# Second attention of a conv-attention hybrid: the mirrored blocks of a chunk's own square turned on VectorE and through memory, and turned tiles stored in pieces and loaded in whole rows

## The chip, the cores and the metric

One core of a Trainium2 chip runs the kernel. The metric is the device time of the program in microseconds (us). TensorE (PE) multiplies matrices, VectorE (DVE), ScalarE (ACT) and GpSimd (POOL) work on tiles, and SyncE (SP) issues most DMAs. Each engine runs its own instructions in order.

## The reference

The input x is 8 batches of 128 channels by 48 x 48 = 2304 positions, in float32. The part that matters here is the second attention; it follows a causal first attention and comes before a recurrent layer.

```python
def _L1_attn_ref(x):                      # x: (8, 2304, 128), normed over its 128 channels
    attn = jnp.einsum('bnd,bmd->bnm', x / TEMPERATURE, x)
    attn = jax.nn.softmax(attn, axis=-1)
    out = jnp.einsum('bnm,bmd->bnd', attn, x)
    return out

x = x + _L0_conv_ref(_gn(x), ...)         # projections, causal attention
t = _to_tokens(x)
t = t + _L1_attn_ref(_ln_t(t))            # the second attention
t = t + _L1_ffn_ref(_ln_t(t), ...)        # batch norm, then a recurrence over positions
```

Queries and keys of the second attention are the same vectors, so its score matrix is symmetric: the score of (n, m) is the score of (m, n). The exponential uses one constant shift for all rows, so the exponentials are symmetric too.

## The kernel before

The 2304 positions of a batch are 6 chunks (`NQ`) of 384 columns (`QC`), and each chunk is 3 blocks (`QB`) of 128. The class `Full` makes the second attention. For a chunk j it takes items: a "direct" item m computes scores of the 128 keys of block m against the chunk's 384 queries (L1214), takes the exponential on ScalarE (L1216, which also adds up each row into `rows`), and multiplies the result `p` into the chunk's output in PSUM, `o` (L1228).

Chunks use the symmetry between one another. A direct item of a later chunk n > j is also turned: VectorE transposes `p` in squares of 32 x 32 into a tile `t` (L1177). After three blocks the tile is complete; its column sums go to `tsum` (L1185), and it is stored in memory (`store`, L1157, one DMA in rows of 4608 bytes) and later loaded back with the squares put in their places (`load`, L1148, four DMAs in pieces of 1152 bytes). When chunk n is worked on, the loaded tile `g` gives a "turned" item, which needs no score and no exponential, only its product (L1224). The three blocks of a chunk's own square (n = j) are all direct, with 384 columns each, and aren't turned. `items` lists the items of each chunk in order: for chunk 0 its own blocks first, for later chunks the blocks behind first and the own ones last, with turned items spread among them.

The products follow the scores by three items (`LAG`). Work around this stream (group norm, projections, the end of a chunk) is written as chains of steps. A planner, `Stream`, keeps estimated times of TensorE, VectorE, ScalarE and GpSimd and puts each step into the instruction stream once its estimated time has come (`tick`); `finish` and `advance` force steps earlier and `finish` moves the planner's clock. The first three items of the next batch's causal attention are placed between the last items of chunk 5.

At the end of a chunk, `after` copies `o` out and adds a chain: `sums` forms the softmax denominators from `rows` and, for chunks with later ones behind them, from `tsum` through a small matmul `ts` (L1259) and the mask `mine`; `residual` turns the result back by TensorE, divides, adds and takes moments; further steps normalize and store.

Buffers that matter: 6 for `p`, 2 for `t`, 3 for `g`, one for `ta` (the causal attention's turned sums) and one for `toc` (the causal attention's output after its way through memory, `token_major`, L961 and L967).

Of the kernel before, what the change touches and what calls it, by code (L numbers as in the profile page):

```python
# [604 lines left out]
def fast_path(ctx: ExitStack, tc: tile.TileContext, x, pe, w_ffn, out, x_tok, w_qkv, w_pos, v_t, gamma_beta, flag):  # L605
    nc = tc.nc
# [57 lines left out]
    with ExitStack() as actx:  # L664
# [91 lines left out]
        for r in range(1 - R, R):  # L756
# [3 lines left out]
        mine = apool.tile([P, NQ - 1, R, QB], F32, tag="mine", name="mine")  # L760
        nc.gpsimd.memset(mine, 1.0)
        nc.gpsimd.affine_select(
            out=mine, in_=mine, compare_op=ALU.is_ge, fill=0.0, base=0, pattern=[[0, NQ - 1], [-SQ, R], [0, QB]], channel_multiplier=1
        )
        nc.gpsimd.affine_select(
            out=mine, in_=mine, compare_op=ALU.is_ge, fill=0.0, base=SQ - 1, pattern=[[0, NQ - 1], [SQ, R], [0, QB]], channel_multiplier=-1
# [351 lines left out]
        class Full:  # L1118
# [13 lines left out]
            def items():  # L1132
                chunks = []
                for j in range(NQ):
                    behind = list(range(j + 1, NQ))
                    ahead = [("direct", QB * n + g) for n in ([0] + behind if j == 0 else behind + [j]) for g in range(QB)]
# [3 lines left out]
                    chunks.append([w for _, w in sorted(both, key=lambda e: e[0])])  # L1140
                return listed(chunks)

            def load(self):
                i, j = self.pairs[len(self.loaded)]
                d, _ = self.stored[i, j]
                g = gpool.tile([P, R, QB, QB, SQ], F32, tag="g", name=f"g_{self.b}_{i}_{j}")
                for r in range(R):
                    nc.sync.dma_start(  # L1148
                        g[ts(r, SQ)].rearrange("c a j m r -> c a (j m r)"),
                        d.rearrange("(a c) b f -> b c a f", a=R)[r],  # L1150
                    )
                self.loaded[i, j] = g

            def store(self):
                j, n, t, at = self.to_store.popleft()
                d = dpool.tile([P, R, QB * QB * SQ], F32, tag=f"e_{j}_{n}", name=f"e_{self.b}_{j}_{n}")
                nc.sync.dma_start(d, t.rearrange("p b j m r -> p b (j m r)"))  # L1157
                self.stored[j, n] = d, max(at, st.now)

            def prefetch(self):  # L1160
# [3 lines left out]
                if n < len(self.pairs) and n < self.used + 3 and self.pairs[n] in self.stored:  # L1164
                    if self.stored[self.pairs[n]][1] + 6.0 <= st.now:
                        self.load()

            def turned(self, j, m, p, ready):
# [12 lines left out]
                if g == QB - 1:  # L1181
                    self.to_store.append((j, n, t, at))
                    if j not in self.tsum:
                        self.tsum[j] = small2.tile([P, NQ - 1, R * QB], F32, tag="tsum", name=f"tsum_{b}_{j}")
                    nc.vector.tensor_reduce(  # L1185
                        self.tsum[j][:, n - j - 1, :], t.rearrange("p b j m r -> p (b j) (m r)"), AX.X, ALU.add
# [4 lines left out]
            def begin(self, j, what, first):  # L1191
# [12 lines left out]
                if what[0] == "turned":  # L1204
# [5 lines left out]
                    return self.loaded[i, j][:, :, g, :, :].rearrange("p a m r -> p m a r"), 0.0  # L1210
                m = what[1]
                xh = x_hat[b][1]
                s = psum_s(f"s1_{b}_{j}_{m}")
                nc.tensor.matmul(s[:, :QC], xh[:, ts(m, P)], xh[:, ts(j, QC)], start=True, stop=True)  # L1214
# [418 lines left out]
```

## Time and profile before

| what | value |
|---|---|
| median of 3 runs | 1776.05 us (1774.83 to 1778.08) |
| span of the profiled execution, first to last instruction | 1772.5 us |
| the profiled execution's own time | not listed; the runs' median is 3.6 us above its span |
| mean granted TensorE clock | 0.993 |
| TensorE busy | 1742.7 us (98%) |
| VectorE busy | 1302.8 us (74%) |
| ScalarE busy | 764.8 us (43%) |
| GpSimd busy | 195.2 us (11%) |
| DMA queue with most traffic | 257.47 MB, 49.4% of 16 engines |

Engines work side by side, so busy times don't add up. In the profile's groups, a line of the kernel stands with its engine, its operation, its output and inputs, the count, the busy time, the mean length of one instruction in ns, and the engine's idle time before them with what ended it. A float32 matmul appears as two MATMUL instructions. Matmuls overlap in the records, so the step from one start to the next tells what one costs in a full stream. The chain of work that ended last is followed back from the last instruction.

### The profile page before, as it was taken

To read this page: it belongs to the slowest core of one execution; us is meant where nothing else is said; L and a number is where in the kernel's file an instruction comes from. 1 tells how busy PE (TensorE), PEld (TensorE's weight loads), DVE (VectorE), ACT (ScalarE), POOL (GpSimd) and SP (SyncE) were. 2 spreads that over 40 slices of the span, in tenths; PEclk is the share of its full clock that TensorE was granted. 3 is DMA by queue.
4 is the path that set the end of the run, shared out by engine and by line. 5 is a ranking of instruction groups with operands and counts; after the bars stand their busy time and mean duration, and the time that the engine had idled before them with its cause. 6 is when DMAs were issued, how large, how long until landed. Compare 5 with 4: busy or idle time off the path is not lost.

```text
span 1772.5 us, 22223 instructions
## 1 busy us (share of the span) xinstructions
PE 1742.7 (98%) x6231; PEld 1093.2 (62%) x6231; DVE 1302.8 (74%) x3363; ACT 764.8 (43%) x1842; POOL 195.2 (11%) x303
## 2 busy tenths in 40 slices
PE   8999999999999999999999999999999999999996
PEld 5666566665666566665666656665666656665565
DVE  4868668876887668786687767876687866877467
ACT  2344434443345434444344433454344543444455
POOL 1110011100110001100111001100011001110006
PEclk8999999999999999999999999999999999999998
DMA  4405672257533584156732575335941468116768
GB/s 140 138 23 187 182 204 94 87 184 188 145 103 128 159 226 141 34 176 182 200 99 80 188 192 152 106 111 161 237 129 50 160 183 214 45 65 198 194 211 216
DMA packets 206056, 262.00 MB, mean 148 GB/s; under 512 B 90113, under 2 KB 175010, under 8 KB 205412
## 3 DMA queue, kind: packets, MB, share of 16 engines
q1 hardware_dynamic: 204972, 257.47, 49.4%
q0 software_dynamic: 720, 2.62, 1.0%
q8 instruction: 52, 0.85, 0.2%
q14 instruction: 80, 0.66, 0.1%
q10 hardware_dynamic: 232, 0.40, 0.1%
HBM read 150.24 MB, written 110.17 MB: 147 GB/s over the span
## 4 chain that ended last, share of the span: by engine, by line
PE 96%; DMA 1%; DVE 1%; ACT 0%; issue 0%; SPq 0%; POOL 0%; ACTq 0%; POOLq 0%; DVEq 0%
PE o L1228 18%; PE s L1214 18%; PE s L1013 17%; PE o L1024 17%; PE o L1224 13%; PE pj L874 4%; PE pj L877 2%; PE z L1547 2%; PE wx L1320 2%; PE of_t L934 1%; PE tb L934 1%; PE pb L832 0%; DMA x<-in_x_dram 0%; PE dn L1072 0%; PE ts L1259 0%
## 5 line engine op out<-in xcount | busy, mean ns | idle before, releaser
L1216 ACT ACTIVATE p<-s,shift 128x384 f32<-128x384 f32 x504 | 292.4, 580 | 479.7 <-PE s L1214 464.2
L1015 ACT ACTIVATE p<-s 128x384 f32<-128x384 f32 (+2 forms) x504 | 231.8, 460 | 424.8 <-PE s L1013 377.5
L1214 PE MATMUL s<-xh 128*128 128x384 f32 x1008 | 410.4, 489 | 0.0
L1228 PE MATMUL o<-p,xhT 128*128 128x384 f32 x1008 | 404.1, 488 | 5.9 <-ACT p L1216 5.9
L1013 PE MATMUL s<-q,k 128*128 128x384 f32 (+2 forms) x1008 | 381.5, 460 | 0.2 <-DVE k L884 0.2
L1024 PE MATMUL o<-p,vT 128*128 128x384 f32 (+2 forms) x1008 | 377.4, 456 | 0.0
L1224 PE MATMUL o<-g,xhT 128*128 128x384 f32 x720 | 281.3, 488 | 1.1 <-DMA g<-e 1.1
L1228 PEld LDWEIGHTS o<-p,xhT 128*128 128x128 f32 x1008 | 188.9, 190 | 133.8 <-ACT p L1216 10.5
L1024 PEld LDWEIGHTS o<-p,vT 128*128 128x128 f32 x1008 | 188.8, 190 | 114.7 <-issue 0.6
L1214 PEld LDWEIGHTS s<-xh 128*128 128x128 f32 x1008 | 186.2, 190 | 115.3
L1013 PEld LDWEIGHTS s<-q,k 128*128 128x128 f32 x1008 | 182.6, 191 | 97.3 <-issue 1.0
L1039 DVE TENSOR_TENSOR acc<-acc,p 128x384 f32<-128x384 f32 (+2 forms) x408 | 208.8, 512 | 33.4 <-POOL p L1018 8.7
L1177 DVE STREAM_TRANSPOSE t<-p 128x384 f32<-128x384 f32 x360 | 187.3, 550 | 37.6 <-ACT p L1216 32.8
L1224 PEld LDWEIGHTS o<-g,xhT 128*128 128x128 f32 x720 | 133.2, 190 | 83.7 <-DMA g<-e 1.3
L1185 DVE TENSOR_REDUCE tsum<-t 128x12 f32<-128x1152 f32 x120 | 162.3, 1353 | 4.2
L879 DVE TENSOR_TENSOR z<-pj,pb 128x384 f32<-128x384 f32 x144 | 78.8, 547 | 108.8 <-PE pj L874 92.4
L1018 POOL TENSOR_TENSOR p<-p,triu 128x128 f32<-128x128 f32 x144 | 72.5, 505 | 606.2 <-ACT p L1015 475.2
L1294 POOL TENSOR_TENSOR roots<-ve_f,mhalf 128x3 f32<-128x3 f32 x48 | 40.7, 849 | 521.8 <-DVE ve_f L918 521.8
L1216 ACT ACTIVATION_READ_ACCUMULATOR p<-s,shift 128x1 f32 x504 | 97.2, 193 | 0.0
L874 PE MATMUL pj<-xn,wT 128*128 128x384 f32 x192 | 79.7, 500 | 1.4 <-DVE xn L867 1.4
L924 POOL TENSOR_TENSOR rs_c<-ve_c,mhalf 128x3 f32<-128x3 f32 x48 | 45.1, 939 | 216.2 <-DVE ve_c L918 213.6
L1321 DVE TENSOR_TENSOR scale<-wx,scale 128x384 f32<-128x384 f32 x46 | 25.4, 551 | 56.1 <-PE wx L1320 50.3
(264 smaller groups left out, 1485.6 us busy)
## 6 DMA issues: line engine op xcount, KB each, us to landing
e<-t SPq DMA_DIRECT2D x120, 576.0 KB
g<-e SPq DMA_DIRECT2D x480, 144.0 KB
pb<-posb_d SPq DMA_DIRECT2D x46, 576.0 KB
t1t<-in_x_tok_dram SPq DMA_DIRECT2D x48, 192.0 KB
t_d<-tt SPq DMA_DIRECT2D x184, 48.0 KB
t2x<-t_d SPq DMA_DIRECT2D x46, 192.0 KB
scale<-rs SPq DMA_DIRECT2D x46, 192.0 KB
x<-in_x_dram SPq DMA_DIRECT2D x14, 576.0 KB
```

Of the source, the lines that this page charges most:

```text
L874: nc.tensor.matmul(ps[:, :QC], wT[:, j, :], xn, start=True, stop=True)
L879: nc.vector.tensor_add(z, ps[:, :QC], c["pb"][:, j, :])
L1013: nc.tensor.matmul(s[:, off:QC], keys[b][:, ts(m, P)], queries[b, j][:, off:], start=True, stop=True)
L1015: nc.scalar.activation(p[:, off:], s[:, off:QC], AF.Exp, scale=SCALE)
L1024: nc.tensor.matmul(o[:, off:QC], vals[b][:, ts(m, P)], p[:, off:], start=first, stop=last)
L1039: nc.vector.tensor_add(a[:, off:], a[:, off:], p[:, off:])
L1177: nc.vector.transpose(t[:, :, :, g, :].rearrange("p b j r -> p j b r"), p.rearrange("p (j b r) -> p j b r", j=QB, b=R))
L1185: nc.vector.tensor_reduce(self.tsum[j][:, n - j - 1, :], t.rearrange("p b j m r -> p (b j) (m r)"), AX.X, ALU.add)
L1214: nc.tensor.matmul(s[:, :QC], xh[:, ts(m, P)], xh[:, ts(j, QC)], start=True, stop=True)
L1216: nc.scalar.activation(p, s[:, :QC], AF.Exp, bias=shift, accum_out=self.rows[:, m, j : j + 1])
L1224: nc.tensor.matmul(out_ap, xhT[:, QB * i + g, :], p, start=first, stop=last)
L1228: nc.tensor.matmul(o[:, :QC], xhT[:, what[1], :], p, start=first, stop=last)
```

## The change

Within a chunk's own square the kernel now computes only the blocks on and behind the diagonal. Own block g gets scores and exponentials for the columns from 128 g on (`offset`): 384, 256 and 128 columns. What lies across the diagonal is obtained by turning: `mirror` transposes the 256 columns of block 0 and the 128 of block 1 in squares of 32 into a tile `tm` (the buffer of `ta`), adds up their columns into `tsum`, stores `tm` in memory and loads it back in four pieces into `gm` (the buffer of `toc`). Two "mirrored" items at the end of the chunk multiply `gm` into the first 128 and 256 columns of `o`.

The own blocks move ahead of the blocks behind in every chunk, and each chunk's first direct item comes first, since it opens the accumulation with its full width. `tsum` has one entry more (the own square), `mine` is one wider, and the last chunk now has the `ts` matmul too.

For the turned tiles of later chunks, the putting in place moves from the load to the store: four stores in pieces of 1152 bytes, and one load in rows of 4608 bytes.

```diff
             def items():
                 chunks = []
                 for j in range(NQ):
-                    behind = list(range(j + 1, NQ))
-                    ahead = [("direct", QB * n + g) for n in ([0] + behind if j == 0 else behind + [j]) for g in range(QB)]
+                    ahead = [("direct", QB * n + g) for n in range(j, NQ) for g in range(QB)]
                     turn = [("turned", i, g) for i in range(j) for g in range(QB)]
                     both = [((k + 0.5) / len(ahead), w) for k, w in enumerate(ahead)]
                     both += [((k + 0.5) / len(turn), w) for k, w in enumerate(turn)]
-                    chunks.append([w for _, w in sorted(both, key=lambda e: e[0])])
+                    order_of = [w for _, w in sorted(both, key=lambda e: e[0])]
+                    first = order_of.index(ahead[0])
+                    order_of.insert(0, order_of.pop(first))
+                    chunks.append(order_of + [("mirrored", g) for g in range(1, QB)])
                 return listed(chunks)
+
+            @staticmethod
+            def offset(j, m):
+                return max(0, m - QB * j) * P if m < QB * (j + 1) else 0
 
             def load(self):
...
-                for r in range(R):
-                    nc.sync.dma_start(
-                        g[ts(r, SQ)].rearrange("c a j m r -> c a (j m r)"),
-                        d.rearrange("(a c) b f -> b c a f", a=R)[r],
-                    )
+                nc.sync.dma_start(g.rearrange("p a j m r -> p (a j m r)"), d.rearrange("p a f -> p (a f)"))
...
             def store(self):
...
-                nc.sync.dma_start(d, t.rearrange("p b j m r -> p b (j m r)"))
+                turned = d.rearrange("(b c) a f -> a c b f", b=R)
+                for r in range(R):
+                    nc.sync.dma_start(turned[r], t[ts(r, SQ)].rearrange("c b j m r -> c b (j m r)"))
...
+            def mirror(self, j, g, p, ready):
+
+                b, left = self.b, QB - 1 - g
+                if g == 0:
+                    if j == 0:
+                        st.advance(normed_chunks[b, NQ - 1], 1)
+                    self.tm = chunk_tile("ta", f"tm_{b}_{j}", bufs=1).rearrange("p (b q r) -> p b q r", b=R, q=QB)
+                first = g * (QB - 1)
+                nc.vector.transpose(
+                    self.tm[:, :, first : first + left, :].rearrange("p b q r -> p q b r"),
+                    p[:, (g + 1) * P :].rearrange("p (q b r) -> p q b r", q=left, b=R),
+                )
+                at = st.then(ready, [("DVE", 0.17 + left * 0.13)])
+                if g < QB - 2:
+                    return
+                ts_own = self.sums_by_column(j)
+                nc.gpsimd.memset(ts_own[:, 0, :, 0], 0.0)
+                nc.vector.tensor_reduce(ts_own[:, 0, :, 1], self.tm[:, :, 0, :], AX.X, ALU.add)
+                nc.vector.tensor_reduce(ts_own[:, 0, :, 2], self.tm[:, :, 1:, :], AX.XY, ALU.add)
+                st.then(at, [("DVE", 0.55)])
+                gm = chunk_tile("toc", f"gm_{b}_{j}", {}, bufs=1).rearrange("p (a q r) -> p a q r", a=R, q=QB)
+                self.gm = gm
+                d = dpool.tile([P, R, QB * SQ], F32, tag=f"m_{j % 2}", name=f"m_{b}_{j}")
+                tm = self.tm
+
+                def out_of():
+                    nc.sync.dma_start(d, tm.rearrange("p b q r -> p b (q r)"))
+
+                def back_in():
+                    for r in range(R):
+                        nc.sync.dma_start(
+                            gm[ts(r, SQ)].rearrange("c a q r -> c a (q r)"), d.rearrange("(a c) b f -> b c a f", a=R)[r]
+                        )
+
+                self.moved = st.add([(out_of, 0.0, [("", 5.0)]), (back_in, 0.0, [("", 5.0)])], at + 0.2 - st.now)
...
+                if what[0] == "mirrored":
+                    st.finish(self.moved)
+                    return self.gm.rearrange("p a q r -> p q a r"), 0.0
                 m = what[1]
+                off = self.offset(j, m)
...
-                nc.tensor.matmul(s[:, :QC], xh[:, ts(m, P)], xh[:, ts(j, QC)], start=True, stop=True)
+                nc.tensor.matmul(s[:, off:QC], xh[:, ts(m, P)], xh[:, j * QC + off : (j + 1) * QC], start=True, stop=True)
...
-                nc.scalar.activation(p, s[:, :QC], AF.Exp, bias=shift, accum_out=self.rows[:, m, j : j + 1])
-                return p, st.then(st.spend(QC * US), [("ACT", 0.58)])
+                nc.scalar.activation(p[:, off:], s[:, off:QC], AF.Exp, bias=shift, accum_out=self.rows[:, m, j : j + 1])
+                return p, st.then(st.spend((QC - off) * US), [("ACT", 0.26 + (QC - off) * 0.00085)])
...
+                elif what[0] == "mirrored":
+                    g = what[1]
+                    cols = g * P
+                    out_ap = o[:, :cols].rearrange("p (m a r) -> p m a r", m=g, a=R)
+                    nc.tensor.matmul(out_ap, xhT[:, QB * j + g, :], p[:, g - 1 : 2 * g - 1], start=first, stop=last)
                 else:
-                    nc.tensor.matmul(o[:, :QC], xhT[:, what[1], :], p, start=first, stop=last)
+                    off = self.offset(j, what[1])
+                    cols = QC - off
+                    nc.tensor.matmul(o[:, off:QC], xhT[:, what[1], :], p[:, off:], start=first, stop=last)
                     st.then(ready, [("ACT", 0.2)])
-                    if what[1] // QB > j:
+                    g = what[1] - QB * j
+                    if g >= QB:
                         self.turned(j, what[1], p, ready)
-                st.spend(QC * US, ready)
+                    elif g < QB - 1:
+                        self.mirror(j, g, p, ready)
+                st.spend(cols * US, ready)
...
-                    n = NQ - 1 - j
-                    if n:
-                        tp = psum_t(f"ts_{b}_{j}")
+                    n = NQ - j
+                    tp = psum_t(f"ts_{b}_{j}")
```

The small matmul, the multiplication with `mine` and the reduction in `sums` are as before, but for every chunk and over `NQ - j` entries.

## The prediction

> **What bounds the kernel now.** I read the busy rows of the page first, then its chain, which says whether a busy engine also sets the end.
>
> ```profile
> PE 1742.7 (98%) x6231; PEld 1093.2 (62%) x6231; DVE 1302.8 (74%) x3363; ACT 764.8 (43%) x1842; POOL 195.2 (11%) x303
> ...
> PE 96%; DMA 1%; DVE 1%; ACT 0%; issue 0%; SPq 0%; POOL 0%; ACTq 0%; POOLq 0%; DVEq 0%
> PE o L1228 18%; PE s L1214 18%; PE s L1013 17%; PE o L1024 17%; PE o L1224 13%; PE pj L874 4%; PE pj L877 2%; PE z L1547 2%; PE wx L1320 2%; PE of_t L934 1%; PE tb L934 1%; PE pb L832 0%; DMA x<-in_x_dram 0%; PE dn L1072 0%; PE ts L1259 0%
> ```
>
> TensorE is busy 98% and carries 96% of the chain; the score and product lines of the second attention (L1214, L1228, L1224) are half of it. A column less on TensorE is time off the end, as long as the stream stays without gaps. Next, what a column costs: the timeline of TensorE, in batch 2's first attention, where 256- and 128-column pieces already stand between full ones (the first two columns are the start and the length in us).
>
> ```profile
> 482.50 0.59 PE L1013 MATMUL s<-q,k 128*128 128x256 f32 x2
> 482.93 0.81 PE L1024 MATMUL o<-p,vT 128*128 128x384 f32 x2
> 483.58 0.81 PE L874 MATMUL pj<-xn,wT 128*128 128x384 f32 x2
> 484.22 0.39 PE L1013 MATMUL s<-q,k 128*128 128x128 f32 x2
> 484.44 0.81 PE L1024 MATMUL o<-p,vT 128*128 128x384 f32 x2
> ...
> 650.87 0.29 PE L1259 MATMUL ts<-tsum,same 128*128 128x12 f32 x2
> 651.01 0.89 PE L1224 MATMUL o<-g,xhT 128*128 128x384 f32 x2
> 651.74 0.81 PE L874 MATMUL pj<-xn,wT 128*128 128x384 f32 x2
> ```
>
> Lengths overlap; starts count. A matmul (two passes) takes 0.645 us of stream at 384 columns, 0.43 at 256, 0.22 at 128: in proportion to columns. The 12-column `ts` takes 0.14 and makes the next start 0.085 late, 0.225 in all. Third, VectorE in the first chunk of batch 2's second attention (windows; columns are stretch, length, PE, PEld, DVE, ACT, POOL, clock, DMA share, GB/s):
>
> ```profile
> 546.00:554.00 8.00, 8.00 (x26) 4.74 (x25) 7.79 (x21) 4.03 (x12) 0.85 (x1) 1.00 0.25 101
> 554.00:562.00 8.00, 8.00 (x28) 4.84 (x27) 7.93 (x15) 4.51 (x13) 0.00 (x0) 1.00 0.82 258
> 562.00:570.00 8.00, 8.00 (x27) 4.78 (x26) 7.12 (x15) 4.17 (x12) 0.00 (x0) 1.00 0.66 232
> 570.00:578.00 8.00, 8.00 (x31) 4.95 (x30) 5.27 (x15) 3.48 (x12) 0.56 (x1) 1.00 0.49 148
> ```
>
> VectorE is full there, without a gap on TensorE: it runs behind (1 to 6 us from the end of an exponential to the turn of the same `p`, matched in the timeline), and the six `p` buffers hold that.
>
> **TensorE's part.** For each of 48 chunks (8 batches of 6) the chunk's own three blocks go from three scores and three products of 384 columns, 6 x 0.645 = 3.87 us, to scores of 384, 256 and 128 (1.295), products of the same (1.295) and two mirrored products of 128 and 256 (0.65): 3.24 us. That is 0.63 x 48 = 30.2 us off; the products keep their columns, and the gain is the scores' missing 384. Against it: the last chunk, which had no turned sums, gets a `ts` matmul, 8 x 0.225 = 1.8 us. Net 28.4.
>
> The short passes are the point where a rule could speak against this. The Trainium skill, page "TensorE: Matmul & The Clock Gate", section "The mechanism" (of packing small matmuls), says that a weight load overlaps running matmuls only where row groups differ; its section "LDWEIGHTS (loading the stationary operand)" prices a load of 128 columns at 107 ns. By that, two more matmuls per chunk would be four exposed loads, an estimate of 0.43 us, and the gain would shrink to about 0.2 us a chunk, some 10 us in all. The starts above show 0.22 us for a whole 128-column matmul with two loads, so the row decides for hidden loads.
>
> **VectorE's part.** Costs come from the groups by form:
>
> ```profile
> L1177 DVE STREAM_TRANSPOSE t<-p 128x384 f32<-128x384 f32 x360 | 187.3, 550 | 37.6 <-ACT p L1216 32.8 <-DMA t_d<-tt 3.6 <-DMA e<-t 1.0
> L1066 DVE TENSOR_REDUCE parts<-ta 128x12 f32<-128x384 f32 x48 | 26.5, 553 | 1.6
> L1299 DVE STREAM_TRANSPOSE roots_t<-roots 128x32 f32<-128x32 f32 x46 | 8.8, 192 | 0.0
> ```
>
> A turn costs 192 ns at 32 and 550 at 384 elements, so about 1.02 ns an element: 290 at 128, 420 at 256. A reduction of 384 takes 553 and one of 12 takes 166 (L1076): 290 and 420 again. The four come to 1.4 us a chunk, 68 us in all; VectorE goes to some 78%. Cover: six `p` buffers. In batch 2 a turn ends at least 1.36 us before the exponential that reuses its buffer, and the product follows its exponential by three items, another 2 us. In chunk 0 the new work is queued before the turns of the later blocks; behind it stand the turned tiles' turns. There the first two turns find gaps (2.73 us before L1074, 0.67 before L1086). Without the cover the price is 1.4 plus 0.63 us in the two full chunks of a batch, 16 x 2 = 32 us. I take 1 us, near the buffers' row. The new `POOL` memset stands between nothing and gn_rs's 0.56 us on an engine 11% busy, but a reduction may wait for it; same cover. ScalarE's exponentials shrink, 383 and 277 ns against 490 in L1015's forms; it has no stake.
>
> **The transfers.** A mirrored chunk adds one store and four quarter loads on SP, the shapes of `o_d_c` and `to_c`:
>
> ```profile
> 665.32 1.01 SPq L961 DMA_DIRECT2D o_d_c<-ot_c  x1
> ...
> 668.25 1.84 SPq L967 DMA_DIRECT2D to_c<-o_d_c  x4
> ```
>
> and SP's own waits (us in total, times, longest):
>
> ```profile
> SPq L967 <- DMA o_d_c<-ot_c: 23.0, 18, 4.8
> ```
>
> A load waited for its store 18 times, 1.3 us on average, 4.8 at worst. From the packet records, the store lands 1.5 us after its issue (5.4 at worst), the four loads 2.9 after the first issue (4.6 at worst): 4.5 us of round trip, 10 at worst. SP issues 2.1 us more a chunk, 100 us over 647 now; what is queued behind the load's wait is tile stores and `g` loads, three pairs ahead of need. For `e` and `g` the 600 issues only change sides. The store in four pieces should land like the `g` quarters, 4.3 us after issue instead of 2.7; the load in whole rows like `pb`, which has its size and rows, 4.1 instead of 4.3. The turned tile has two buffers, so a full VectorE wants the first one back 4.0 us after its third turn (1.35 reduction, three turns, 1.35): up to 0.3 us a tile in chunk 0, within the cover above.
>
> The loads have 384-byte pieces. The Trainium skill, page "DMA: Bandwidth & Descriptors", section "Specifications", asks for 512 bytes or more for full rate. In the packet records 384 bytes take 26 ns and 1152 take 76, the same per byte, so I add nothing.
>
> Who waits for the mirrored block? In chunks 0 to 4 its products come at least 13 items after the turn (10 us or more). In chunk 5 the second own block is item 8 of 20, and between its product and mirrored product 1 stand nine products (5.4 us), its neighbour's score (0.2), the next batch's first three scores and products (2.6) and two scores (1.3): 9.5 us, beside inserted projections. The need is 4.5 plus VectorE's lateness (0.1 to 5.3 us in chunk 4). It just fits; bounds 0 and, with the worst store (5.4), load (4.6) and lag (6.4), 16.4 - 9.5 = 7 us a batch. I take 0.25 us, 2 in all, near the median round trip. In batch 7 no next batch follows: 5.6 us, where the tail already stands still 3 us; I add 1.
>
> The planner allows the trip 5 us each way. In chunk 5 its own sum for the same stretch is shorter by up to 3 us, so `finish` sets its clock ahead by that and puts the following steps into TensorE's stream that much early. I price this at nothing: the steps that wait for DMAs are planned with 10 us (`spread`) and 9 us (`fetch`), where transfers of this size landed 4 us after their issue. Without that cover it is 8 x 3 = 24 us.
>
> At the start of chunks 4 and 5 only turned and mirrored products (0.645 + 0.22 + 0.43 = 1.3 us) lie between the first score and its product, where 1.9 lay before; a score at 1683.85 had its exponential ready 1.5 us after its start, which is 0.85 after its slot. It fits unless a 1.13 us copy (L1326, L1341) stands ahead on ScalarE; bounds 0 and 16 x 1, I take 2. A 0.63 us gap of that sort is there now in each batch (615.33) and may go or stay: 5 us below nothing.
>
> **Sum.** 30.2 - 1.8 - 1 - 3 - 2 = 22.4 us. The page gives the profiled execution a span of 1772.5 us; its whole time isn't listed, and the runs' median of 1776.05 is 3.6 above that span, which I take as what lies around it. 1772.5 - 22.4 = 1750.1 of span, 1753.7 of time.
>
> **Rivals.**
> (a) New waits eat most of the gain without a single owner: VectorE full in chunks 0 and 1 gives nothing back there (16 x 0.63 = 10) and chunk 5 waits 1 us a batch where I took 0.25 (6 more): 1753.7 + 10 = 1764 with the first, 1770 with both. For it: the 7.93 of 8. Against: TensorE has no gap there although VectorE is late.
> (b) Slower: in chunk 5 the mirrored load comes too late. Out and back stand on SP in program order, the load blocked until the store lands, with `rs`, `t_d` and tile stores around them that wait for VectorE. Past 9.5 + 3.5 = 13 us from turn to landing, all 28.4 us are gone; at the bound of 16.4 us the time is 1776 - 28.4 + 56 = 1804. For it: tile stores wait up to 25.2 us for VectorE on SP. Against: those waits are for work not yet due, and 4.5 us is the usual trip.
> (c) VectorE decides chunks 0 and 1 at full price: 1776 - 28.4 + 32 = 1780, no clear change. Against: 3.4 us of cover.
> (d) The change doesn't skip scores: the diff cuts both operands to `off:`, so only hidden loads could fail, which the 0.22 us start excludes.
>
> **Numbers.** Forecast 0.78; (a) 0.10; (b) 0.08; (c) 0.04. The likeliest is 1753.7. Low: no new wait and the old gaps gone, 1776.05 - 28.4 - 5 = 1743; high: into (a), 1768. Two in a thousand (about 3.5 us) is what a measurement here can tell from nothing: faster 0.87, same 0.05, slower 0.08.
>
> **What would show it.** Scores of the second attention in three widths, 504 of them as before, and 96 mirrored products; TensorE's busy time down by about 28 us; VectorE up by about 68; the period of a batch, 207.7 us now, near 204.5. Wrong: idle time before the mirrored products ended by a DMA, or before own products ended by ScalarE; chunk 0 longer with VectorE at 8.0 of 8.

## The result: no change where 22 us were forecast, and the profile after

Over twelve interleaved runs each, the kernel before takes 1776.2 us (1774.0 to 1778.1) and the changed one 1776.86 us (1770.7 to 1780.6). The ratio is 1.0006, 95% interval 0.9995 to 1.0017: the same. The profiled execution of the changed kernel has a span of 1768.9 us and took 1770.66 us, the fastest of its twelve. So 1.8 us lie around a span (not the 3.6 that the prediction inferred), and a typical execution of the changed kernel takes some 6 us more than the one read here.

The page of the changed kernel, busy rows and chain:

```profile
PE 1722.4 (97%) x6439; PEld 1110.7 (63%) x6439; DVE 1362.0 (77%) x3579; ACT 744.4 (42%) x1842; POOL 206.7 (12%) x351
...
PE 91%; DMA 5%; DVE 2%; SPq 1%; ACT 0%; issue 0%; POOL 0%; ACTq 0%; DVEq 0%; POOLq 0%
PE s L1013 17%; PE o L1024 17%; PE s L1262 16%; PE o L1284 16%; PE o L1272 11%; PE pj L874 3%; DMA g<-e 3%; PE o L1280 2%; PE z L1605 2%; PE pj L877 2%; PE wx L1378 2%; PE tb L934 1%; PE of_t L934 1%; PE pb L832 0%; SPq L1161 0%; DMA pb<-posb_d 0%
```

TensorE has less work, but its share of the chain falls from 96% to 91%, and 5% are now DMAs, 3% of them the load `g<-e`, which was not in the chain before. (In the changed file the score is L1262, the direct product L1284, the turned product L1272, the mirrored one L1280; the tile store is L1161, the tile load L1153.) The matmul groups of the page (the last field is idle time before them and what ended it):

```profile
L1262 PE MATMUL s<-xh 128*128 128x384 f32 (+2 forms) x1008 | 382.0, 461 | 4.5 <-ACT xh L1105 4.5
...
L1284 PE MATMUL o<-p,xhT 128*128 128x384 f32 (+2 forms) x1008 | 373.3, 458 | 0.0
L1272 PE MATMUL o<-g,xhT 128*128 128x384 f32 x720 | 282.3, 491 | 17.4 <-DMA g<-e 17.3
```

The same groups before:

```profile
L1214 PE MATMUL s<-xh 128*128 128x384 f32 x1008 | 410.4, 489 | 0.0
L1228 PE MATMUL o<-p,xhT 128*128 128x384 f32 x1008 | 404.1, 488 | 5.9 <-ACT p L1216 5.9
L1224 PE MATMUL o<-g,xhT 128*128 128x384 f32 x720 | 281.3, 488 | 1.1 <-DMA g<-e 1.1
```

Two waits are new. Before, the turned product waited 1.1 us in all and the score not at all; now the first waits 17.3 us for its tile, the second 4.5 us for `xh`. One old wait went: the 5.9 us of the direct product for `p`.

**Where the 28 us went.** From the starts of TensorE's matmuls between 60 and 1700 us I added up by how much each start came later than the one before it plus its price in a full stream (0.645 us for a pair of passes at 384 columns, and so on; only delays over 0.15 us). The kernel before loses 9.5 us in this way, the changed one 33.2: 19.2 in twelve waits for `g`, 5.9 in eight for `xh` (0.73 each, one a batch), 1.5 in one for `xhT`, 0.9 for `gm`, the rest mostly matmuls at half clock. The forecast 28.4 us less work, minus 33.2 - 9.5 = 23.7 us more waiting, is 4.7; the spans differ by 3.6.

**Why a tile comes late.** The timeline of SP in batch 2's chunk 4 (start, length, tile, number of issues; `rs`, `t_d` and `t2c` are what the ends of chunks store, and pair (i, j) is the tile that chunk i turned for chunk j):

```profile
614.33 1.99 SPq L1208 DMA_DIRECT2D gm<-m  x4
616.36 2.24 SPq L1363 DMA_DIRECT2D rs<-roots_t  x3
620.08 1.74 SPq L1366 DMA_DIRECT2D t_d<-tt  x4
621.91 1.82 SPq L1161 DMA_DIRECT2D e<-t  x4
623.84 0.39 SPq L1153 DMA_DIRECT2D g<-e  x1
624.33 0.56 SPq L1408 DMA_DIRECT2D out_dram<-t2c  x1
624.93 3.73 SPq L1409 DMA_DIRECT2D t2l_d<-t2c  x1
628.75 2.04 SPq L1161 DMA_DIRECT2D e<-t  x4
630.89 0.39 SPq L1153 DMA_DIRECT2D g<-e  x1
```

and of TensorE at the tile that the last of these loads:

```profile
632.67 0.81 PE L1272 MATMUL o<-g,xhT 128*128 128x384 f32 x2
635.39 0.91 PE L1272 MATMUL o<-g,xhT 128*128 128x384 f32 x2 [1.91 <-DMA g<-e]
```

The buffer for this tile was released at 623.85, by the last product of the tile three before it. Its load went out at 630.89, 7.0 us later: from 614 to 631 SP issues with one longer stop, 1.5 us ahead of `t_d` that a DMA ended; it is behind by what stands there, and between the release and this load it still has another load, the two stores of `t2c` and a tile's four stores to issue. It has 4.5 us to land, and TensorE stands 1.91 us. Over the eight batches the median time from the released buffer to the load of pair (2,4) is 6.4 us, where it was 2.7 before; for (1,4) 4.3 against 3.3, for (2,5) 2.7 against 1.2. A load takes 4.1 us to land (median in chunks 4 and 5, 4.4 before), so a longer flight is not the reason.

**The wait for `xh`** is in chunk 0 of every batch:

```profile
556.52 0.49 PE L934 MATMUL tb<-ident,xhT 128*128 128x128 f32 x3
557.58 0.91 PE L1262 MATMUL s<-xh 128*128 128x384 f32 x2 [0.57 <-ACT xh L1105]
```

The step that turns the last causal chunk back (`tb`) is forced by `finish` right ahead of the score that needs its `xh`; ScalarE's copy lies between, and the score waits. Before, `tb` stood between earlier scores and nothing waited.

**Half clock.** Two stretches of 3.41 us in the middle of the changed kernel's span run at a granted clock of 0.5; the kernel before has none there. The second follows a wait of 4.4 us for `g`, the first one for `xhT` and one for `xh` (timeline of TensorE):

```profile
348.90 0.75 PE L934 MATMUL tb<-ident,xhT 128*128 128x128 f32 x3 [1.38 <-DVE xhT L929]
350.22 0.97 PE L1262 MATMUL s<-xh 128*128 128x384 f32 x2 [0.57 <-ACT xh L1105]
350.99 1.48 PE L1284 MATMUL o<-p,xhT 128*128 128x384 f32 x2
352.27 1.48 PE L1262 MATMUL s<-xh 128*128 128x384 f32 x2
```

The starts are 1.28 us apart instead of 0.645. Such a stretch costs about 1.7 us, and it makes waits dearer than they are.

### The profile page after: what moved, and what is told of

The parts are those of the page before. It is cut to its first block, busy times and chain, and to the rows that moved or that the text cites. A ratio compares the mean times of both kernels' runs of the same rounds, so it can differ in the third digit from the quotient of the medians.

```text
span 1768.9 us, 23170 instructions
## 1 busy us (share of the span) xinstructions
PE 1722.4 (97%) x6439; PEld 1110.7 (63%) x6439; DVE 1362.0 (77%) x3579; ACT 744.4 (42%) x1842; POOL 206.7 (12%) x351
## 4 chain that ended last, share of the span: by engine, by line
PE 91%; DMA 5%; DVE 2%; SPq 1%; ACT 0%; issue 0%; POOL 0%; ACTq 0%; DVEq 0%; POOLq 0%
PE s L1013 17%; PE o L1024 17%; PE s L1262 16%; PE o L1284 16%; PE o L1272 11%; PE pj L874 3%; DMA g<-e 3%; PE o L1280 2%; PE z L1605 2%; PE pj L877 2%; PE wx L1378 2%; PE tb L934 1%; PE of_t L934 1%; PE pb L832 0%; SPq L1161 0%; DMA pb<-posb_d 0%
## 5 line engine op out<-in xcount | busy, mean ns | idle before, releaser
L1264 ACT ACTIVATE p<-s,shift 128x384 f32<-128x384 f32 (+2 forms) x504 | 277.1, 550 | 543.1 <-PE s L1262 511.1
L1262 PE MATMUL s<-xh 128*128 128x384 f32 (+2 forms) x1008 | 382.0, 461 | 4.5 <-ACT xh L1105 4.5
L1284 PE MATMUL o<-p,xhT 128*128 128x384 f32 (+2 forms) x1008 | 373.3, 458 | 0.0
L1272 PE MATMUL o<-g,xhT 128*128 128x384 f32 x720 | 282.3, 491 | 17.4 <-DMA g<-e 17.3
L1284 PEld LDWEIGHTS o<-p,xhT 128*128 128x128 f32 x1008 | 189.7, 191 | 118.5 <-issue 1.2
L1262 PEld LDWEIGHTS s<-xh 128*128 128x128 f32 x1008 | 183.5, 191 | 104.0 <-ACT xh L1105 6.4
L1272 PEld LDWEIGHTS o<-g,xhT 128*128 128x128 f32 x720 | 131.1, 190 | 97.5 <-DMA g<-e 26.7
L1018 POOL TENSOR_TENSOR p<-p,triu 128x128 f32<-128x128 f32 x144 | 77.0, 535 | 586.1 <-ACT p L1015 560.6
```

Source lines behind the costliest of these rows:

```text
L1262: nc.tensor.matmul(s[:, off:QC], xh[:, ts(m, P)], xh[:, j * QC + off : (j + 1) * QC], start=True, stop=True)
L1264: nc.scalar.activation(p[:, off:], s[:, off:QC], AF.Exp, bias=shift, accum_out=self.rows[:, m, j : j + 1])
L1272: nc.tensor.matmul(out_ap, xhT[:, QB * i + g, :], p, start=first, stop=last)
L1284: nc.tensor.matmul(o[:, off:QC], xhT[:, what[1], :], p[:, off:], start=first, stop=last)
```

## The experiments

The theory from the profile, G: TensorE's saving is real and is spent in waiting for `g`, and SP's order holds the loads. Rivals: the layout of the transfers (P), the mirrored round trip's own load on SP (M), the order of items (O), the place of the mirrored items in chunk 0 (C). Ratios are to the kernel before, run beside each; "delays" are the sum explained above.

**1. The changed kernel with rows out and pieces in, as before the change.**

```diff
-                nc.sync.dma_start(g.rearrange("p a j m r -> p (a j m r)"), d.rearrange("p a f -> p (a f)"))
+                for r in range(R):
+                    nc.sync.dma_start(
+                        g[ts(r, SQ)].rearrange("c a j m r -> c a (j m r)"),
+                        d.rearrange("(a c) b f -> b c a f", a=R)[r],
+                    )
...
-                turned = d.rearrange("(b c) a f -> a c b f", b=R)
-                for r in range(R):
-                    nc.sync.dma_start(turned[r], t[ts(r, SQ)].rearrange("c b j m r -> c b (j m r)"))
+                nc.sync.dma_start(d, t.rearrange("p b j m r -> p b (j m r)"))
```

> The change with one part undone: turned tiles go out in whole rows (one store) and come back in pieces (four loads), as before the change. Theory P (pieces: four store issues now stand ahead of a due load on SP, and this makes the load late): TensorE's waits for g, 17 us in the profile after, fall to 3 or less, and the time is about 1777 - 15 = 1762 us. Theory M (the mirrored block's own five DMAs and the wait between its store and loads fill SP, whichever side the pieces are on): waits for g stay at 10 us or more, time 1772 to 1778. Theory O (the order with own blocks first puts tile stores later, beside the loads): the same as M here.

1794.39 us, ratio 1.0102 (1.0087 to 1.0116). Delays 50.6: `g` 21.8, `gm` 10.6. P falls: stores in pieces don't hurt; without them the change would have been 1% slower.

**2. The layout alone, on the kernel before.**

> The kernel before with one part of the change alone: turned tiles stored in four pieces and loaded in one DMA of whole rows; scores, items and order as before. Theory P: loads stand behind four store issues, waits for g of 10 us or more, time 1785 to 1790 us. Theories M and O: nothing new on SP, since the issues only change sides; within 2 us of 1776.

1774.3 us, 0.9997 (0.9988 to 1.0005): worth nothing there. Undoing it cost time only in the changed kernel, where TensorE waits for loads (run 1).

**3. Without the round trip.** The mirrored store and loads are left out, and `gm` is filled with a constant by GpSimd, so the mirrored products use no turned values.

```diff
-                self.moved = st.add([(out_of, 0.0, [("", 5.0)]), (back_in, 0.0, [("", 5.0)])], at + 0.2 - st.now)
+                nc.gpsimd.memset(gm.rearrange("p a q r -> p (a q r)"), 0.5)
...
-                    st.finish(self.moved)
```

> The change without the mirrored block's way through memory: the store and the four loads are left out and gm is filled with a constant by GpSimd, so the mirrored products take data that isn't the mirrored block; all else, turns and sums included, stays. Theory M: SP has five issues and one wait for a landing less per chunk; waits for g fall from 17 us to 3 or less, time about 1777 - 15 = 1762 us. Theories P and O: waits for g stay at 10 us or more, time 1772 to 1778. In all theories the 0.73 us wait for xh in each batch's chunk 0 stays.

1776.82 us, 1.0009 (0.9996 to 1.0021). M falls as the whole cause: with 240 issues fewer the wait for `g` is the same in size and elsewhere, now seven waits of 2.2 us in chunk 5 and one of 0.7 in chunk 4. Load by load, the trip did hold chunk 4: without it the load of pair (2,4) goes out 1.6 us (median) after its buffer came free, against 6.4. In chunk 5 that of (2,5) now goes out 3.6 us after, against 2.7. SP in batch 2, where this buffer came free at 643.41:

```profile
641.52 1.57 SPq L1362 DMA_DIRECT2D rs<-roots_t  x3
643.13 1.86 SPq L1365 DMA_DIRECT2D t_d<-tt  x4
645.09 1.82 SPq L1161 DMA_DIRECT2D e<-t  x4
647.01 0.39 SPq L1153 DMA_DIRECT2D g<-e  x1
```

So `t_d` and a tile's store stand right ahead of the late load here.

**4. The mirrored items of chunk 0 ahead of its last three direct items.**

```diff
+                    at = len(order_of) - QB if j == 0 else len(order_of)
+                    chunks.append(order_of[:at] + [("mirrored", g) for g in range(1, QB)] + order_of[at:])
```

> The change with the two mirrored items of chunk 0 placed ahead of its last three direct items instead of behind them; nothing else. Theory C (chunk 0's gain is lost at the first score that needs the last causal chunk's xh, which comes at a time of its own): that wait, 8 x 0.73 = 5.9 us in the profile after, goes to 0.1 us or less a batch, and the time falls by 4 to 6 us to about 1772. Rival (the wait follows VectorE's lateness and only moves to the next item): no change, within 2 us of 1777.

1788.67 us, 1.0082 (1.0069 to 1.0096). The `xh` wait is as it was (8 x 0.77), so C falls; the waits for `g` grow to 27.0 us. The move touches no load, and yet the waits for loads grew.

**5. The tile loads issued by ScalarE** (`nc.scalar.dma_start` in `load`).

> The change with the loads of turned tiles issued by ScalarE's queue instead of SP's; stores and all else stay on SP. Theory Q (SP issues in program order, and due loads stand behind stores, the ends of chunks and the mirrored block's DMAs: in batch 2 the load of pair (2,4) was issued 7.0 us after its buffer came free, that of (2,5) 2.6 us after): loads follow their buffers within 1 us, TensorE's waits for g fall from 17 us to 3 or less, and the time is about 1777 - 16 = 1761 us. Theory R (three buffers and 4.3 us of landing are too little for chunks 4 and 5 however soon the load is issued): waits for g stay above 8 us and the time above 1768 us. Rival (ScalarE is held up by the loads' waits and its exponentials come late): slower than 1777 us, with TensorE waiting for p.

1852.44 us, 1.0436 (1.0404 to 1.0468). The wait for `g` falls to 2 us, but others take its place. From SP's waits and TensorE's waits of this kernel:

```profile
SPq L1161 <- DMA g<-e: 115.9, 39, 6.1
```

```profile
PE o L1280 <- DMA gm<-m: 25.9, 11, 5.7
PE wx L1378 <- DMA t2x<-t_d: 18.2, 6, 4.1
```

With all 120 loads in another queue, SP's next stores wait for them by the profile (115.9 us, against 7.5 in the changed kernel), and the mirrored and second-chain transfers are late instead.

**6. The order of items alone, on the kernel before** (own blocks first in every chunk).

> The kernel before with the new order alone: the chunk's own blocks ahead of the blocks behind, the first direct item first; all scores in full width, no mirrored items. Theory O (tile stores come three items later and stand beside the loads of chunks 4 and 5): waits for g of 8 us or more and a time of 1784 us or more. Theory Q with the mirrored DMAs or the shorter chunks as what overfills SP: no new waits, within 2 us of 1776.

1774.36 us, 0.9996 (0.9987 to 1.0004): O falls. The `xh` delay is there already (5.1 us in seven waits) without a loss in total; that for `g` stays at 1.2.

**7. Chunk 4's own blocks last again** (`if j == NQ - 2: ahead = ahead[:1] + ahead[QB:] + ahead[1:QB]`).

> The change with chunk 4 alone in another order: its first own block, then the three blocks behind, then the other two own blocks, so that the store of the last turned tile, pair (4,5), leaves chunk 5. Theory O: chunk 5's waits for g (about half of the 17 us) go, against up to 0.5 us a batch of wait for gm in chunk 4; time about 1777 - 6 = 1771 us. Theories Q (other DMAs) and R: within 2 us of 1777, or later by the wait for gm.

1835.58 us, 1.0342 (1.0319 to 1.0365). The mirrored products now follow their turn too closely: 26.1 us of delay for `gm`, and 16.6 for `g` remain.

**8. Run 5 with `xh` made early in chunk 0** (the edit of run 11).

> As the loads on ScalarE's queue, and chunk 0 has the last causal chunk's xh turned back one product earlier (the planner's step is forced four blocks ahead at the product, not at the score that needs it). Theory C2 (the 0.73 us wait in chunk 0 is that step's place in TensorE's stream): a further 4 to 5.5 us off the kernel with the loads on ScalarE's queue, about 1756 us by theory Q. Rival (VectorE's norm itself is late): the wait moves to that step and 2 us or less are gained.

1839.65 us, 1.0378 (1.0356 to 1.0400): 12.8 us under run 5, and the `xh` delay falls from 5.9 to 2.6.

**9. One tile load a batch.** Fourteen of fifteen loads in a batch are left out, and every turned product takes the first tile.

```diff
+                if self.loaded:
+                    self.loaded[i, j] = self.loaded[0, 1]
+                    return
```

> The change with all but the first of a batch's 15 loads of turned tiles left out: every turned product takes that first tile, so the data of the others isn't theirs; stores, mirrored blocks, items and order stay. Theory G (the gain is spent on TensorE waiting for loads of turned tiles, and on the half clock that follows such a wait): no waits for g, 19 us of them and about 2 us of half clock gone, so about 1777 - 20 = 1757 us. Rival (the next thing is late at once: p, gm or the ends of chunks take the waits over): 1770 us or more, with the waits under another name.

1748.89 us, 0.9848 (0.9833 to 0.9863). From its page:

```profile
PE 97%; DVE 1%; DMA 1%; ACT 0%; SPq 0%; issue 0%; POOL 0%; DVEq 0%; ACTq 0%; POOLq 0%
...
L1275 PE MATMUL o<-g,xhT 128*128 128x384 f32 x720 | 278.1, 488 | 0.0
```

Delays 10.9, of which `xh` 5.9; no half clock in mid-span. The first half of G holds: some 27 us of gain were there and were spent at this one wait and the half clock behind it. Run 9 also takes 112 issues off SP, so it doesn't show what made the loads late.

**10. Run 9 with early `xh`.**

> As the kernel with one load per batch (14 of 15 loads of turned tiles left out), and the last causal chunk's xh turned back one product earlier. If waits for g and the wait for xh in chunk 0 are all that ate the 28 us, this shows the gain of TensorE's part: about 1757 - 5 = 1752 us, 24 us under the kernel before. If something else bounds the batch, it stays above 1765 us.

1741.5 us, 0.9810 (0.9796 to 0.9823): 7.4 us below run 9, more than the 3.4 us that the delay for `xh` fell by.

**11. The changed kernel with early `xh` alone.**

```diff
+                    if j == 0:
+                        st.finish(normed_chunks[self.b, min(what[1] + 4, NB - 1) // QB])
                     off = self.offset(j, what[1])
```

> The change with nothing but the last causal chunk's xh turned back one product earlier in chunk 0. If the two losses add up one by one: 4 us less, about 1773 us. If time gained ahead of chunks 4 and 5 is lost again there, since their loads come when SP's program order lets them: waits for g grow by what is gained and the time stays within 2 us of 1777.

1763.5 us, 0.9931 (0.9919 to 0.9944): it beats both kernels. `xh` 2.5 us instead of 5.9, `g` 15.8 instead of 19.2, one `xhT` wait less. It gained 13 us where its own wait explains 3.4; the rest was not taken apart. Some of it is the choice of executions: the two profiled ones, the fastest of the changed kernel and the slowest of this one, are 5.3 us apart, and their delays (33 and 28) differ by about as much.

**12. Run 11 with the mirrored trip planned 7 us later in chunks 0 to 3, and the stores of `t2c` issued by GpSimd.**

> The change with three edits that could beat both kernels: xh one product earlier in chunk 0; the mirrored loads of chunks 0 to 3 placed 7 us later on SP, so that SP needn't stand still for the store's landing (94 us over the run in the profile after); and the residual's two stores of each batch (t2c; 3.7 us of issue on SP in chunk 4) moved to GpSimd's queue. Theory Q (SP's program order makes the loads late): waits for g fall to 8 us or less, time 1760 to 1766 us. Rival (three buffers and the landing time bound chunk 5 however SP is relieved): waits for g stay above 14 us, time above 1770 us.

1883.08 us, 1.0622 (1.0599 to 1.0646). TensorE's waits:

```profile
PE o L1280 <- DMA gm<-m: 84.3, 32, 6.4
PE o L1024 <- ACT p L1015: 4.4, 7, 0.9
PE o L1272 <- DMA g<-e: 2.7, 6, 0.9
```

The later place makes the mirrored load late in 32 of 48 chunks. Two edits at once, and the first hides what the second does; the next runs move one thing each.

**13. Run 11 with the two stores of `t2c` (L1408, L1409) issued by GpSimd.**

> The kernel of the early `xh` (1763.5 us) with the two stores of `t2c` at the end of the second attention's fourth chunk of residuals (L1410 and L1411: 0.56 and 3.73 us of SP's issue time in the changed kernel's profile) issued by GpSimd, whose queue then holds them and not SP's. All else stays on SP. Theory 'these two stores stand ahead of the loads': they cost one stop of SP of 4.3 us in each of 8 batches, the wait of L1272 on `g<-e` of chunk 4 falls from some 2 us in a batch to under 0.5 and the time by 8 to 16 us, to 1748 to 1756. Theory 'SP is behind as a whole': the loads go out by at most 4 us sooner for one pair of a batch, and the time falls by 2 to 6 us. Theory 'any move of a transfer makes another wait': the same or slower.

1759.6 us, 0.9913 (0.9887 to 0.9939): 3.9 us below run 11, but the two intervals overlap, so this gain isn't clear of noise. `g` 8.5, but `gm` 4.0.

**14. Run 11 with the rows of `tt` (L1366) issued by GpSimd.**

```diff
-                        nc.sync.dma_start(d[r], c["tt"][ts(r, SQ)].rearrange("c (k f) -> c k f", k=R))
+                        nc.gpsimd.dma_start(d[r], c["tt"][ts(r, SQ)].rearrange("c (k f) -> c k f", k=R))
```

> The kernel of the early `xh` (1763.5 us) with the four stores of `tt` into `t_d`'s rows (L1366, `d[r]`, four issues in each of 48 chunks of the second chain, each of which waits on SP for VectorE's transposition) issued by GpSimd. Theory 'SP stands at stores that wait for VectorE': SP's wait of these four goes to GpSimd (busy 12%), the loads behind them go out at once, the wait of L1272 on `g<-e` falls from 14 us to under 5 and the time by 8 to 15 us, to 1748 to 1756. Theory 'any move makes another wait': GpSimd's product with the triangle (L1018) stands behind the wait and TensorE waits for `p`: the same or slower.

1744.66 us, 0.9833 (0.9806 to 0.9861): 18.8 us below run 11, the fastest kernel here that leaves nothing out. `g` 0.7 us in one wait. The expected reason, stops of SP for VectorE at these stores, is not borne out: SP's waits at them in run 11 were ended by DMAs, 9.9 us in all, and none by VectorE. What they take is SP's time: four issues a chunk, and these stops.

**15. Run 11 with the mirrored trip issued by GpSimd.**

> The kernel of the early `xh` (1763.5 us) with the mirrored blocks' store and its four loads (L1206 and L1210, five issues in a chunk, in all 48 chunks) issued by GpSimd. On SP they took 94 us of wait of the loads for the store's landing and 172 us of wait of the store for VectorE's sums, each a stop of the whole queue. Theory 'the stops of the trip hold SP': the wait of L1272 on `g<-e` falls from 14 us to under 5, the time by 8 to 15 us, to 1748 to 1756, the mirrored products do not wait. Theory 'any move makes another wait': GpSimd's other steps (the triangle of `p`, the roots) stand behind the trip's stops and the time is the same or more.

1764.7 us, 0.9941 (0.9921 to 0.9962): no better than run 11, although 240 issues left SP. TensorE's waits, where run 11 has 14.1 us for `g` and 0.6 for `gm`:

```profile
PE o L1280 <- DMA gm<-m: 10.5, 9, 2.7
PE o L1272 <- DMA g<-e: 3.6, 4, 2.3
```

**16. Runs 13 and 14 together.**

> The two moves of stores together, on the kernel of the early `xh`: the stores of `t2c` and the rows of `tt` by GpSimd, the mirrored trip and the tiles' stores and loads by SP. If both stand ahead of the loads, the gains add up: g waits under 2 us in all and a time of 1740 to 1748, near the 1741.5 us of the kernel that loads one tile in a batch. If any move makes another wait, the time lies above 1760.

1751.49 us, 0.9872 (0.9845 to 0.9900): 6.8 us above run 14 alone, with `gm` 4.3 and `g` 2.9. The gains don't add up.

**17. The changed kernel with run 14's edit and nothing else.**

> The changed kernel (1776.9 us) with the four stores of `tt` a chunk issued by GpSimd and nothing else; the `xh` wait stays. Theory 'SP's order held the loads': the wait of L1272 on `g<-e` falls from 17 us to under 2, and the time by some 20 us, to 1750 to 1757, which is what the prediction's sum gave without a wait for transfers. Theory 'the early `xh` is needed too' (the two work only together): 1762 to 1774.

1750.97 us (1747.9 to 1752.1), 0.9864 (0.9850 to 0.9879). Busy row, chain and the turned product on its page:

```profile
PE 1715.0 (98%) x6439; PEld 1110.0 (64%) x6439; DVE 1362.9 (78%) x3579; ACT 744.3 (43%) x1842; POOL 310.2 (18%) x535
...
PE 96%; DMA 2%; DVE 1%; ACT 0%; SPq 0%; issue 0%; POOL 0%; DVEq 0%; ACTq 0%; POOLq 0%
...
L1272 PE MATMUL o<-g,xhT 128*128 128x384 f32 x720 | 278.3, 488 | 0.4 <-DMA g<-e 0.4
```

SP's timeline in batch 2's chunk 4 has the same items but for `t_d`, which GpSimd issues after its roots (second view, GpSimd):

```profile
612.89 0.40 SPq L1408 DMA_DIRECT2D out_dram<-t2c  x1
613.34 2.58 SPq L1409 DMA_DIRECT2D t2l_d<-t2c  x1
616.01 2.03 SPq L1161 DMA_DIRECT2D e<-t  x4
618.14 0.39 SPq L1153 DMA_DIRECT2D g<-e  x1
```

```profile
627.56 0.88 POOL L1352 TENSOR_TENSOR roots<-ve_f,mhalf 128x3 f32<-128x3 f32 x1 [19.22 <-DVE ve_f L918]
628.41 2.22 POOL L1366 DMA_DIRECT2D t_d<-tt  x4
```

The load of pair (2,4) goes out 2.6 us after its buffer came free (615.58), where the changed kernel took 7.0; the medians are 2.8 and 6.4. When the buffer comes free SP has 0.3 us of the stores of `t2c` left to issue; in the changed kernel both were still to come. SP's issue times add up to 657 us in 1454 issues, where they were 750 in 1638 in the changed kernel and 647 in 1398 before. The delays are 13.1 us, with `xh` at 5.9 and `g` at 0.6.

**18. The same move on the kernel before.**

> The kernel before (1776.2 us) with the same move alone: the four stores of `tt` a chunk by GpSimd. If the move is worth something by itself, whatever the mirrored blocks do, this is 10 to 20 us faster as well, and the change is worth little even with SP relieved. If SP's order binds only with the mirrored transfers and the faster TensorE, nothing waits for SP in the kernel before (1.2 us on `g<-e`), and this stays within 3 us of 1776.

1772.79 us (1771.0 to 1775.5), 0.9988 (0.9979 to 0.9997): 2.5 us less than the kernel before beside it (1775.32). So the move is worth 2.5 us without the change and 25.9 with it (25.2 by the ratios, since the changed kernel was timed in another session), and the change, on a relieved SP, is worth 1772.79 - 1750.97 = 21.8 us.

## Why the prediction was wrong

**The step that failed** is in "The transfers": "SP issues 2.1 us more a chunk, 100 us over 647 now; what is queued behind the load's wait is tile stores and `g` loads, three pairs ahead of need." The 100 us are right (750 were measured) and were priced at nothing, by a cover that was not there. Three buffers are three pairs ahead only if the load goes out when a buffer comes free. In the kernel before that took 2.7 us for pair (2,4), then 4.4 to land, with 7.3 us (median) from issue to use: less than 3 us to spare. For pair (2,5) the load landed after 3.6 of the 5.8 us to its use: 2.2 to spare. The view that would have shown it is the timeline of SP beside that of TensorE in chunks 4 and 5, by load: released, issued, used. I read the waits of SP in total and did not measure that margin. On top of that, each chunk saves TensorE 0.63 us and its tiles are wanted that much sooner. It cost 19.2 us in the profiled execution; runs 9 and 17 remove it in two unlike ways, and both come to some 1750 us. The added issues alone don't explain it: without them (run 3) chunk 4's loads are on time and chunk 5's are late, behind `t_d`.

**What I did not price at all**: the wait for `xh` in chunk 0, 5.9 us. The prediction asked what the new order does to the products at chunk starts, and not which planned step `finish` forces ahead of a score there. The new order alone brings it (run 6).

**TensorE's part: right.** Busy time was to fall by 28; it falls by 27.7 in run 17 (1742.7 to 1715.0) and by 20.3 in the changed kernel, whose matmuls are stretched by half clock and waits. The 128-column matmuls cost what was forecast: from start to start a pass takes 0.111 us (median of 96 mirrored ones), 0.22 for the two, so no weight load is exposed. The period of a batch, from the first exponential of one to that of the next, was to fall from 207.7 us to 204.5: run 17 has 204.4 on average, the changed kernel 206.7, from 205.2 to 209.4.

**VectorE's part: right.** The forms of the new work in the changed kernel's groups:

```profile
L1186 DVE STREAM_TRANSPOSE tm<-p 128x256 f32<-128x256 f32 x48 | 20.7, 431 | 3.2 <-ACT p L1264 2.1
L1196 DVE TENSOR_REDUCE tsum<-tm 128x4 f32<-128x256 f32 x48 | 19.5, 406 | 0.0
L1186 DVE STREAM_TRANSPOSE tm<-p 128x128 f32<-128x128 f32 x48 | 13.6, 284 | 5.2 <-ACT p L1264 5.2
L1195 DVE TENSOR_REDUCE tsum<-tm 128x4 f32<-128x128 f32 x48 | 11.8, 245 | 0.0
```

They add up to 65.6 us, 68 forecast; VectorE's busy time rose by 59.2. VectorE is as full in chunk 0 as before (windows):

```profile
545.00:553.00 8.00, 8.00 (x32) 5.04 (x31) 7.28 (x22) 4.39 (x13) 0.90 (x2) 1.00 0.49 118
553.00:561.00 8.00, 7.43 (x26) 4.36 (x25) 7.93 (x14) 3.84 (x11) 0.00 (x0) 1.00 0.80 180
```

and the 0.57 us that TensorE lacks in the second row are the `xh` wait, which no VectorE work ended. Rival (c) did not occur.

**The mirrored trip: its time too short, its cover longer.** In chunk 5 the four loads have been issued 6.8 us after the turn (median), and they still have to land, so the 4.5 us for the whole trip were too few; but the first mirrored product starts 12.6 us after the turn, where I counted 9.5. It cost 0.9 us, not 3, and rival (b) did not occur. Runs 7 and 12 show how little is to spare: with the product sooner the delay is 26 us, with the trip later 76.

**ScalarE at the starts of chunks 4 and 5**: priced at 2 us, not seen; the old gap of 5.9 us that "may go or stay" went.

**Rivals.** The result is of the kind of (a), new waits that eat the gain, but with one main owner, in chunks 4 and 5, and larger: 23 us where (a) counted 10 to 16. The condition in the prediction's list of what would make it wrong named mirrored and own products; the wait was at the turned ones.

**The sum after all**: 22.4 us net were forecast and 21.8 measured between runs 17 and 18. That is partly luck, since `xh` (5.9) stood in for terms that did not occur.

**What stays open.** The move of `t_d` takes 79.8 us of issue time from SP, and it also changes the transfer: by the page's queues, an issue leaves as 32 packets of 1536 bytes in the second queue, instead of 128 of 384 bytes in SP's. The load of pair (2,4) then goes out 3.5 us sooner. How long a late load flies did not change: by the packet records it lands after 4.4 us (median; 4.3 before the move) for (2,4) and after 4.3 us (4.3) for (2,5). So what counts is when it goes out. Whether SP gets there sooner only by the issues it no longer has, or also because the other packets changed, wasn't run apart; the issue of `t2l_d` became shorter too, 2.9 us on average instead of 3.6. Taking 240 issues of the mirrored trip off SP (run 15) helps so much less than taking 184 issues of `t_d` because the wait moves: that for `g` falls by 10.5 us and that for `gm` rises by 9.9. On GpSimd the trip waits for VectorE and for its own store; which of the two makes `gm` late is open.

## What to carry to other kernels

Before pricing DMAs that are added to an issuing queue at nothing, take the transfers that the bound engine consumes and read for each when its buffer came free, when it was issued, when it landed and when it was used: the smallest margin is the price list, and a faster engine shortens it. If a kernel is saved work and stays as slow, leave the suspected transfers out once (run 9) to see whether the gain exists, and then move one group of issues at a time to an idle engine. Moving more, or moving the transfers that the bound engine waits for, only changed who waits (runs 5, 12, 15 and 16).

## What the runs showed of the hardware that was not expected

- The engine that issues a DMA can decide the time where bandwidth does not: 184 issues on GpSimd instead of SP were worth 25.9 us, with 281 MB moved in both. The Trainium skill, "DMA: Bandwidth & Descriptors", section "Issuing engines are not separate DMA queues", says that another engine only saves the issuing time, "which is usually small relative to the DMA itself". The first half fits. Issue by issue the second mostly fits too: a `t_d` issue on GpSimd took 0.56 us of the 3.4 us (median) to landing, though one of `t2l_d` held SP for 2.1 to 4.9 us in the changed kernel. In sum it was not small: SP's 1638 issues take 750 of the 1769 us.
- An issue is dearer on GpSimd, 0.56 us against 0.43 us for the same `t_d` piece on SP (103.0 and 79.8 us over 184), and TensorE waited for none of it in run 17, on an engine that was 12% busy before.
- The clock halved after waits far shorter than its window. The Trainium skill, "TensorE: Matmul & The Clock Gate", section "What's actually happening", gives an idle window of about 3.4 us as the condition. The stretches at half clock are 3.41 us long, as there; but the windows of this trace show TensorE busy 1.43 of the 2.90 us ahead of one (the first row below, third field), so half-idle was enough there. It isn't always: after a stretch with 1.59 of 3.41 us busy (from 1248.65) the clock stayed full. The two rows:

```profile
348.00:350.90 2.90, 1.43 (x5) 0.91 (x6) 2.87 (x8) 0.48 (x1) 0.00 (x0) 1.00 1.00 223
350.90:354.30 3.40, 3.40 (x7) 1.78 (x6) 1.65 (x2) 1.18 (x4) 0.00 (x0) 0.51 0.93 300
```
